# Attention and mixture of experts on one core: the weighted sums of two head groups in one PSUM bank, and the row maxima's transposes at the head of a step

## The chip, the core and the metric

The kernel runs on one core of a Trainium2 chip. The metric is the time of one execution on the device, in microseconds; less is better. A core has a matrix engine (TensorE, PE in the profile, its weight loads PEld), a vector engine (VectorE, DVE), an engine for activation functions (ScalarE, ACT), a general engine (GpSimd, POOL) and SyncE (SP), which here only starts DMA transfers. PE reads SBUF and writes PSUM, which has eight banks of 512 fp32 numbers in each of 128 partitions. The engines run their own queues in order, and wait for each other through semaphores.

## What is computed

Eight sequences of 512 tokens with 128 features. Rows are normalised; the result is the input plus causal attention with 16 heads of 8 dimensions, plus a shared feed-forward block, plus the two best of eight expert blocks for each token.

```python
x = L0_attn_x                       # 8 x 512 x 128
xn = _layernorm(x, axis=-1)
x = x + _L0_attn_ref(xn, ...) + _L0_ffn_ref(xn, ...)

# attention
h = (x @ W1 + b1).reshape(B, S, H, 3 * d)          # H = 16, d = 8
w = einsum('bhqd,bhkd->bhqk', q, k) / sqrt(d)
w = softmax(w * mask - (1 - mask) * 1e6)
a = einsum('bhqk,bhkd->bhqd', w, v)
return a @ Wp + bp

# feed-forward: FF = 352, eight experts, two of them for each token
_ffn = silu(x @ gw.T) * (x @ uw.T) @ dw.T
topw, topi = top_k(softmax(xf @ gate_w.T), 2);  topw = topw / topw.sum()
return shared + sum over experts of _ffn(xf, expert) * its weight
```

## The kernel before

Everything is written out in one order per engine: PE, DVE, ACT and SP take their instructions as the program records them; only POOL's order is left to a scheduler. The 16 heads of a sequence are four groups of four heads, so that there are 32 groups n (`b, g = divmod(n, NG)`). A group is five steps (`TILES`): two "wide" ones, two "mixed" ones and one "half" one, 160 steps in all.

In a step, in this order (the loop at L1092 to L1138):

- `begin(step)` runs what an earlier step has left for the head of this one (the lists in `first`).
- `weigh` fills a pair of banks with scores (`fill`, L308 and the mask's product L312), and ACT takes their exponential into `pT` (L428). From step 33 on and until the routed blocks are done, POOL cuts the causal triangle out of `pT` (L436) in place of the mask's product.
- `look` computes scores for a later group, query rows on the partitions (`peak_scores`, L351 into `sc_left` and `sc_diag`), and DVE reduces them to row maxima (`peaks`, L380 and L386). It is 7 steps ahead at first and 11 from step 24 on. After a group's fifth look, `shift_parts` (L394 to L403) makes of the maxima three bf16 parts.
- `some_chunks` does a chunk of the feed-forward work beside it: `chunk` (two products `gu`, L584; tanh on ACT, L589; two DVE operations `th` and `h`, L590 and L591). There is one PSUM buffer for `gu`.
- `late` holds what the step before has left: `attend`, the weighted sums (L451), and at the end of a group `evacuate` (L475).
- `side` runs what is due in this step (`ready`), then up to two pieces of feed-forward work: `down` (y, L602, copied by ACT to `o`, L610, or added by DVE, L613) or `turn_slots` (s_ps, L568, copied to `sT`, L570).

The weighted sums of a group are four strips of 32 partitions in one bank, `av`: strip jj belongs to head jj of the group. The stationary operand is `v_ext[b % NV][:, c, head, :]`, 32 columns wide: columns 0 to 7 are the head's values, column 8 is 1, so that row 8 of a strip is the softmax's denominator, and columns 9 to 31 are zero. `project_v` copies the values into it, once for each sequence (L277). After a group's last sums, ACT copies the bank to `o_sb` (L475); two steps later `divide` turns it with four transposes (`ot`, L484), and DVE takes the reciprocals of the denominators (`rden`, L486) and multiplies (`a_new`, L490). When a sequence's four groups are divided, `turn` (L498, L499) and `join` (L521, L525) multiply by Wp and add to x.

The maxima's parts go into the query operand as three more rows: `shift` (L409) turns the parts on PE into `mT_ps`, DVE copies them (L411), and `put_shift` starts three DMAs on SP (L416). For groups 4 and up `shift` is due at the second step after the fifth look, in `side`, near the end of that step; `side` then leaves `put_shift` for the head of the next step:

```python
        return lambda: due(step + (2 if n > 3 else 1), partial(shift, n, shift_parts(n)))
```

The products `qk_ps`, `v_ps`, `ot`, `mT_ps`, `y`, `s_ps`, `aT_ps` and `p_ps` share two PSUM buffers of one bank each (`misc`). On SP stand, beside the three DMAs of a shift, the loads of expert weights (L542, 576 KB each, two for a pair of blocks, with six buffers), of the rows of a pair of blocks (L553), and of queries and keys (L285, L287).

The routing is done once, in the first steps; then POOL scatters the rows to the experts' slots (`send`, L649, 64 scatters), and at the end gathers the results (`collect`, L662), which DVE weights and adds (L669). Before the routed blocks and after them the shared block fills the chunks.

Of the kernel before, what the change touches and what calls it, by code (L numbers as in the profile page):

```python
# [11 lines left out]
F32 = mybir.dt.float32  # L12
# [3 lines left out]
ALU = mybir.AluOpType  # L16
# [9 lines left out]
P = 128  # L26
B, S, E = 8, 512, 128
H, D = 16, 8
NC = S // P
NT = B * NC  # L30
NG = H // 4
HH = H // 2
NU = 3
NV = 2
# [28 lines left out]
def attn_moe_kernel(  # L63
# [15 lines left out]
    nc = tc.nc  # L79
# [52 lines left out]
    for i in range(NU):  # L132
        q = const.tile([P, HH, S], BF16, name=f"qs{i}")
        k = const.tile([P, HH, S], BF16, name=f"ks{i}")
# [3 lines left out]
    def ones_below(k):  # L138
        nc.gpsimd.memset(k[64:96].rearrange("p h s -> p (h s)").bitcast(F32), PAIR_OF_ONES)

    ones_below(ks[0])
    for t in v_ext:
        nc.gpsimd.memset(t, 0.0)
        nc.gpsimd.memset(t[:, :, :, D : D + 1], 1.0)


    mask_q = const.tile([P, P], BF16, name="mask_q")
# [48 lines left out]
    def pool(name, bufs, **kw):  # L196
        return ctx.enter_context(tc.tile_pool(name=name, bufs=bufs, **kw))
# [3 lines left out]
    at = pool("at", 2)  # L201
# [68 lines left out]
    def project_v(b):  # L270
        ps = misc([P, NC, H, D], "v_ps")
        for c in range(NC):
            nc.tensor.matmul(
                ps[:, c].rearrange("p h d -> p (h d)"),
                lhsT=xnT[:, ts(b * NC + c, P)], rhs=w1v_sb, start=True, stop=True,
            )
        nc.scalar.copy(v_ext[b % NV][:, :, :, :D], ps)  # L277

    def fetch(u, h0=0, h1=HH):

# [132 lines left out]

    def put_shift(n, mT):
        for r in range(3):
            d = nc.sync.dma_start(  # L416
                qs[n // 2 % NU][QK + r : QK + r + 1, ts(n % 2, 4), :].rearrange(
                    "o h (c s) -> o (h c) s", s=P
                ),
                mT[ts(r, 16)],  # L420
            )
        return d.ins

    def weigh(n, kind, j, on_pool):

# [16 lines left out]
    def attend(n, tiles, av):  # L442

        b, g = divmod(n, NG)

        def add(jj, c, weights):  # L450
            nc.tensor.matmul(  # L451
                av[32 * jj : 32 * jj + 32, c * P :], lhsT=v_ext[b % NV][:, c, 4 * g + jj, :],
                rhs=weights, start=(c == 0), stop=(c == NC - 1), skip_group_check=True,
            )

        heads = [(j + t, pT[:, t]) for _, j, pT in reversed(tiles) for t in range(2)]
        kind = tiles[0][0]
        if kind == "wide":
            for jj, w in heads:
                add(jj, 0, w)  # L460
        elif kind == "mixed":
            for jj, w in heads:
                add(jj, 1, w[:, : 3 * P])
            for jj, w in heads:
                add(jj, 3, w[:, 3 * P :])
        else:
            for t, w in heads:
                for u in range(2):
                    add(2 * t + u, 2, w[:, ts(u, 2 * P)])
# [8 lines left out]
    def divide(n):  # L478

        b, g = divmod(n, NG)  # L480
        o_sb = group_sums.pop(n)
        ot = misc([P, NC, 4, 32], "ot")
        for c in range(NC):
            nc.tensor.transpose(ot[:, c].rearrange("p j s -> p (j s)"), o_sb[:, ts(c, P)], ident)  # L484
        rden = at.tile([P, NC, 4, 1], F32, name="rden")
        nc.vector.reciprocal(rden, ot[:, :, :, D : D + 1])  # L486
        if g == 0:
            a_new = at.tile([P, NC, E], F32, name="a_new")
            a_sb[b] = a_new
        nc.vector.tensor_tensor(  # L490
            a_sb[b][:, :, ts(g, 4 * D)].rearrange("p c (j d) -> p c j d", d=D),
            ot[:, :, :, :D], rden.to_broadcast([P, NC, 4, D]), ALU.mult,
        )

    def turn(b):
# [35 lines left out]
    weights, held, turned, hidden = {}, {}, {}, {}  # L531
# [149 lines left out]
    late = []  # L681
# [3 lines left out]
    def due(step, f):  # L685
        ready.setdefault(step, []).append(f)
# [3 lines left out]
    def look(step, between=lambda: None):  # L690

        t = len(looked)
        if t >= total_steps:
            return lambda: None
        looked.append(step)
        n, i = divmod(t, NTILES)
        maxima(n, i, between)
        if i < NTILES - 1:
            return lambda: None
        if n == 0:  # L700
            return partial(shift_parts, n)
        return lambda: due(step + (2 if n > 3 else 1), partial(shift, n, shift_parts(n)))

    def side(step, most):

# [6 lines left out]
    first = {}  # L712
# [5 lines left out]

    def begin(step):
        for f in first.pop(step, []):  # L720
            f()

    def extra():
        do, more = next(beside, (None, []))
# [325 lines left out]
    for t in range(FIRST):  # L1050
        step = t - FIRST
# [40 lines left out]
    for n in range(B * NG):  # L1092
        b, g = divmod(n, NG)
        waiting = []
        for i, (kind, j) in enumerate(TILES):
            step = n * NTILES + i
            begin(step)
            if step in fetches:
                fetch(fetches[step])
            on_pool = step >= BUSY and len(stored) < NB // MB  # L1100
            waiting.append((kind, j, weigh(n, kind, j, on_pool)))
            parts_then = look(step)
            some_chunks(step, False)
            if step in light:
                warm(5)
            parts_then()
            if step not in MORE and len(looked) < total_steps:
                prepare(*divmod(len(looked), NTILES))
            some_routing()
            for f in late:  # L1110
                f()
            late = []
            if i == 1:
                av = av_ps.tile([P, S], F32, name="av")
            if i in (1, 3, 4):
                late = [partial(attend, n, waiting, av)]
                waiting = []
            side(step, 2)
            some_chunks(step, True)
            if step in MORE:  # L1120
                look(step)()
                prepare(*divmod(len(looked), NTILES))
            if len(stored) == NB // MB:
                for _ in range(2 + (step % 3 == 0)):
                    if gathers:
                        t, i_ = gathers.pop(0)
                        collect(t, i_)
                        due(step + LAG, partial(add_up, t, i_))

                        if i_ and t % NC == NC - 1 and t < MB * EARLY:  # L1130
                            due(max(step + LAG + 1, last_shift), partial(store, t // NC))
        late.append(partial(evacuate, n, av))
        due(step + 2, partial(divide, n))
        if n % NG == 2 and b + 1 < B:
            due(step + 1, partial(offset, b + 1))
        if g == NG - 1:
            due(step + 3, partial(turn, b))
            due(step + 4, partial(join, b))  # L1138
    for f in late:
        f()  # L1140
    while aside or beside is not None:
        do, more = next(beside, (None, []))
# [8 lines left out]
    for step in sorted(ready):  # L1151
        for f in ready[step]:
            more = f()
# [12 lines left out]
def _lay_out(inp):  # L1166

    import numpy as np

    a = {k: np.asarray(v) for k, v in inp.items()}  # L1170
    w1 = a["L0_attn_W1"].reshape(E, H, 3 * D)
    b1 = a["L0_attn_b1"].reshape(H, 3 * D)

    def by_dim(v):
        return np.swapaxes(v, -1, -2).reshape(*v.shape[:-2], D * H)

    def experts(name):
        return np.concatenate([a[f"L0_ffn_expert_{name}"], a[f"L0_ffn_shared_{name}"][None]], axis=0)

    pad = ((0, 0), (0, 0), (0, FP - FF))  # L1180
    w_gate = np.pad(experts("gate").transpose(0, 2, 1), pad)
    w_up = np.pad(experts("up").transpose(0, 2, 1), pad)
    w_down = np.pad(experts("down"), pad)
    w_down = w_down.reshape(NE + 1, E, NF, P).transpose(0, 3, 2, 1).reshape(NE + 1, P, FP)

    arrays = {
        "x": a["L0_attn_x"],
        "w1q": by_dim(w1[:, :, :D]),
        "w1k": by_dim(w1[:, :, D : 2 * D]),
        "bq": by_dim(b1[:, :D]).reshape(P, 1),  # L1190
        "bk": by_dim(b1[:, D : 2 * D]).reshape(P, 1),
        "w1v": w1[:, :, 2 * D :].reshape(E, H * D),
        "bv": b1[:, 2 * D :].reshape(H * D, 1),
        "wp": a["L0_attn_Wp"],
        "bp": a["L0_attn_bp"].reshape(1, E),
        "gate_w": np.pad(a["L0_ffn_gate_w"].T, ((0, 0), (0, GATES - NE))),
        "w_exp": np.concatenate([w_gate, w_up, w_down], axis=2),
    }
    return {f"in_{k}_dram": np.ascontiguousarray(v) for k, v in arrays.items()}
# [17 lines left out]
```

## Time and profile before

| | |
|---|---|
| median of 5 runs | 679.61 us |
| lowest, highest | 677.07, 685.84 us |
| the profiled execution's own time | 678.34 us |
| its span, first to last instruction | 676.6 us |
| mean granted TensorE clock | 0.946 of full speed |
| busy: PE, DVE, ACT, POOL | 575.3, 453.3, 380.2, 240.4 us |
| instructions | 13710 |

The page of the profile gives the busy time of each engine, then the span in 40 slices of 16.9 us with the busy share in tenths, then the chain of work that ended last, then the groups of instructions by line. A group's row reads: line, engine, operation, result <- operands, shapes, count, then the busy time of the group and the mean duration of one in ns, then the time for which the engine had been idle just before them, and for whom it had waited. PE's records overlap, since its matmuls are pipelined: the time from one start to the next start is what one costs, not its duration. An fp32 matmul is recorded as two, a transpose as one. A row of the timeline reads: start, duration, engine, line, what, how many; in brackets how long the engine had been idle before it, and for whom.

### The profile page before, as it was taken

The numbers are of one execution on the slowest core, as the hardware profiler recorded it, in microseconds if no ns is written. First come the engines' busy times: TensorE is split into PE (matmuls) and PEld (weight loads), VectorE is DVE, ScalarE is ACT, GpSimd is POOL, SyncE is SP. The second block draws the span as 40 slices with busy tenths as digits, with TensorE's granted clock in tenths as the row PEclk, the third lists the DMA queues.
The fourth block names the chain that finished last, engine by engine and source line by source line (L and its number), as shares of the span: only waits on it lengthen the run. The fifth ranks groups of instructions, "written<-read, shape, count | busy, mean of one in ns | idle before, by whom it ended". The sixth has DMA issues, their size and how long they took to land.

```text
span 676.6 us, 13710 instructions
## 1 busy us (share of the span) xinstructions
PE 575.3 (85%) x4946; PEld 423.7 (63%) x4946; DVE 453.3 (67%) x1172; ACT 380.2 (56%) x676; POOL 240.4 (36%) x350
## 2 busy tenths in 40 slices
PE   7888892019999999999999989999999999869995
PEld 4564661016767777777777767777877776546653
DVE  7788681017777766767666666677767777769952
ACT  5635351006565666667556675667656676535552
POOL 9313777770000222222222212221222212777750
PEclk9989697559999999999999999999999999969999
DMA  7671532110426668586776659575775723432250
GB/s 201 205 230 72 161 103 74 50 47 25 111 71 143 173 196 219 160 215 185 198 234 182 199 160 208 188 190 182 226 214 176 222 77 87 96 77 54 56 154 16
DMA packets 51533, 98.71 MB, mean 146 GB/s; under 512 B 10137, under 2 KB 35609, under 8 KB 49305
## 3 DMA queue, kind: packets, MB, share of 16 engines
q1 hardware_dynamic: 43912, 79.52, 42.3%
q0 software_dynamic: 6832, 18.23, 8.2%
q8 instruction: 39, 0.64, 0.4%
q14 instruction: 30, 0.24, 0.1%
q10 hardware_dynamic: 720, 0.08, 0.1%
HBM read 73.29 MB, written 24.12 MB: 144 GB/s over the span
## 4 chain that ended last, share of the span: by engine, by line
PE 62%; POOL 11%; DVE 9%; ACT 7%; issue 7%; DMA 3%; SPq 0%; POOLq 0%; DVEq 0%; ACTq 0%
PE gu L584 19%; PE y L602 10%; PE av L451 9%; POOL slots L649 9%; PE scT L308 8%; PE sc_diag L351 4%; PE sc_left L351 4%; DVE peaks L380 2%; PE qk_ps L228 2%; ACT th L589 2%; ACT pT L428 2%; PE s_ps L568 2%; DVE th L590 2%; DMA r<-results,slot 2%; DVE h L591 1%
## 5 line engine op out<-in xcount | busy, mean ns | idle before, releaser
L428 ACT ACTIVATE pT<-scT 128x1024 f32<-128x1024 f32 x160 | 163.8, 1024 | 66.2 <-PE scT L312 52.8
L584 PE MATMUL gu<-sT,w 128*128 128x128 f32 x864 | 116.8, 278 | 13.3 <-DVE h L591 7.9
L436 POOL TENSOR_SCALAR_AFFINE_SELECT pT<-pT 128x256 f32<-128x256 f32 (+1 forms) x130 | 55.1, 436 | 194.3 <-ACT pT L428 194.2
L584 PEld LDWEIGHTS gu<-sT,w 128*128 128x128 f32 x864 | 107.5, 191 | 21.1 <-PE sc_left L351 10.1
L380 DVE TENSOR_REDUCE peaks<-sc_diag 128x4 f32<-128x512 f32 x128 | 87.9, 687 | 46.4 <-PE sc_diag L351 43.1
L308 PE MATMUL scT<-qs,ks 75*128 75x384 bf16 (+3 forms) x512 | 107.4, 304 | 5.5 <-ACT pT L428 5.4
L339 ACT CAST sc_diag<-mask_q 128x512 f32<-128x512 bf16 x117 | 69.3, 592 | 71.2 <-DVE peaks L380 58.6
L590 DVE SCALAR_TENSOR_TENSOR th<-th,gu 128x256 f32<-128x256 f32 x156 | 65.4, 419 | 58.2 <-ACT th L589 56.0
L589 ACT ACTIVATE th<-gu 128x256 f32<-128x256 f32 x156 | 59.8, 383 | 71.7 <-PE gu L584 71.3
L451 PE MATMUL av<-pT,v_ext 128*32 128x512 f32 (+3 forms) x1024 | 90.5, 449 | 0.2 <-ACT pT L428 0.2
L351 PEld LDWEIGHTS <-qs 72*128 72x128 bf16 x896 | 64.9, 99 | 37.7 <-issue 20.9
L380 DVE TENSOR_REDUCE peaks<-sc_left 128x4 f32<-128x512 f32 x128 | 87.1, 681 | 0.0
L649 POOL DMA_INDIRECT slots<-rows_attT,slot x64 | 62.9, 982 | 33.7 <-issue 17.1
L351 PE MATMUL sc_diag<-ks,qs 72*128 72x128 bf16 (+1 forms) x576 | 62.9, 227 | 13.4 <-ACT sc_diag L339 11.9
L591 DVE TENSOR_TENSOR h<-gu,th 128x256 f32<-128x256 f32 x156 | 66.2, 424 | 5.4
L602 PE MATMUL y<-ws_sb,h 128*128 128x128 f32 x192 | 29.7, 294 | 47.0 <-DVE x_sb L613 44.2
L662 POOL DMA_INDIRECT r<-results,slot x64 | 61.3, 958 | 23.1 <-issue 9.9
L602 PE MATMUL y<-w,h 128*128 128x128 f32 x432 | 63.2, 283 | 5.7 <-ACT sT L570 1.6
L602 PEld LDWEIGHTS y<-w,h 128*128 128x128 f32 x432 | 54.2, 191 | 18.5 <-issue 3.9
L351 PE MATMUL sc_left<-ks,qs 72*128 72x128 bf16 (+1 forms) x320 | 62.4, 277 | 3.3 <-DVE peaks L380 3.1
L308 PEld LDWEIGHTS <-ks 75*128 75x128 bf16 x512 | 49.4, 100 | 19.8 <-issue 8.2
L602 PEld LDWEIGHTS y<-ws_sb,h 128*128 128x128 f32 x192 | 25.4, 199 | 54.3 <-DVE x_sb L613 44.4
(159 smaller groups left out, 716.2 us busy)
## 6 DMA issues: line engine op xcount, KB each, us to landing
w<-in_w_exp_dram SPq DMA_DIRECT2D x72, 576.0 KB
qs<-dq SPq DMA_DIRECT2D x45, 192.0 KB
ks<-dk SPq DMA_DIRECT2D x45, 192.0 KB
slots<-zeros POOLq DMA_DIRECT2D x6, 768.0 KB, 5.8
results<-o POOLq DMA_DIRECT2D x36, 128.0 KB, 7.1
s<-slots SPq DMA_DIRECT2D x33, 128.0 KB
dq<-parts SPq DMA_DIRECT2D x7, 384.0 KB
dk<-parts SPq DMA_DIRECT2D x7, 384.0 KB
```

Source lines behind the costliest of these rows:

```text
L308: nc.tensor.matmul(out_, lhsT=k[: QK + 3, ts(i, P)], rhs=q[: QK + 3, i * P :], start=True, stop=bare)
L339: nc.scalar.copy(diag_ps.rearrange("p (b k) -> p b k", k=P), mask_q.unsqueeze(1).to_broadcast([P, NC, P]),)
L351: nc.tensor.matmul(out_, lhsT=q[:QK, ts(c, P)], rhs=k[:QK, keys], start=start, stop=stop, skip_group_check=True,)
L380: nc.vector.tensor_reduce(peaks[:, i, 8 + 4 * t : 12 + 4 * t], banks[t].rearrange("p (b k) -> p b k", k=P), AX.X, ALU.max,)
L428: nc.scalar.activation(pT, ps, AF.Exp, scale=D**-0.5)
L451: nc.tensor.matmul(av[32 * jj : 32 * jj + 32, c * P :], lhsT=v_ext[b % NV][:, c, 4 * g + jj, :], rhs=weights, start=(c == 0), stop=(c == N ...
L584: nc.tensor.matmul(gu[:, i, part], lhsT=w[c][:, ds(i * FP + f * P, P)], rhs=sT[:, part], start=True, stop=True,)
L589: nc.scalar.activation(th, gu[:, 0], AF.Tanh, scale=0.5)
L590: nc.vector.scalar_tensor_tensor(th, th, 1.0, gu[:, 0], ALU.add, ALU.mult)
L591: nc.vector.tensor_tensor(h[:, f], gu[:, 1], th, ALU.mult)
L602: nc.tensor.matmul(y, lhsT=h[:, f, ts(c, P)], rhs=w[c % len(w)][:, ds(2 * FP + f * P, P)], start=(f == 0), stop=(f == NF - 1),)
L649: d = nc.gpsimd.indirect_dma_start(slots, bass.IndirectOffsetOnAxis(ap=slot[:, i, t : t + 1], axis=0), rows[:, t, :], None,)
```

## The change

One bank now holds the sums of two groups. Groups with an even number write into it as before; for odd groups the values stand 16 columns further right in `v_ext`, so that their sums and denominator come into rows 16 to 24 of each strip, and the zero columns add nothing to the rows of the other group. The bank is opened by the even group's first matmul and closed by the odd group's last. It is copied to `o_sb` and divided once for two groups, after the odd one: four transposes, one reciprocal of 128x32 and one product of 128x256 in place of twice four, two of 128x16 and two of 128x128. The order of the heads in the result changes with it, and `bv` and `wp` are laid out to match on the host (`by_sums`). The values are copied into `v_ext` by two copies of 128x256 in place of one of 128x512, and the ones are set by two memsets for each of the two `v_ext` in place of one.

For groups 4 and up the shift is put at the head of the step in whose `side` it was due: transpose, copy and the three DMAs are all recorded in `begin`.

```diff
+    def halves_of(t):
+        return t.rearrange("p c (q t j) s -> p (c q) t j s", t=2, j=4)
...
-        nc.gpsimd.memset(t[:, :, :, D : D + 1], 1.0)
+        for i in range(2):
+            nc.gpsimd.memset(halves_of(t)[:, :, i, :, 16 * i + D : 16 * i + D + 1], 1.0)
...
-        nc.scalar.copy(v_ext[b % NV][:, :, :, :D], ps)
+        for i in range(2):
+            nc.scalar.copy(
+                halves_of(v_ext[b % NV])[:, :, i, :, 16 * i : 16 * i + D], halves_of(ps)[:, :, i]
+            )
...
-                rhs=weights, start=(c == 0), stop=(c == NC - 1), skip_group_check=True,
+                rhs=weights, start=(n % 2 == 0 and c == 0), stop=(n % 2 == 1 and c == NC - 1),
+                skip_group_check=True,
...
-        ot = misc([P, NC, 4, 32], "ot")
+        ot = misc([P, NC, HH, 16], "ot")
         for c in range(NC):
-            nc.tensor.transpose(ot[:, c].rearrange("p j s -> p (j s)"), o_sb[:, ts(c, P)], ident)
-        rden = at.tile([P, NC, 4, 1], F32, name="rden")
+            nc.tensor.transpose(ot[:, c].rearrange("p k s -> p (k s)"), o_sb[:, ts(c, P)], ident)
+        rden = at.tile([P, NC, HH, 1], F32, name="rden")
         nc.vector.reciprocal(rden, ot[:, :, :, D : D + 1])
-        if g == 0:
+        if g == 1:
...
-            a_sb[b][:, :, ts(g, 4 * D)].rearrange("p c (j d) -> p c j d", d=D),
-            ot[:, :, :, :D], rden.to_broadcast([P, NC, 4, D]), ALU.mult,
+            a_sb[b][:, :, ts(g // 2, HH * D)].rearrange("p c (k d) -> p c k d", d=D),
+            ot[:, :, :, :D], rden.to_broadcast([P, NC, HH, D]), ALU.mult,
...
-        return lambda: due(step + (2 if n > 3 else 1), partial(shift, n, shift_parts(n)))
+        if n < 4:
+            return lambda: due(step + 1, partial(shift, n, shift_parts(n)))
+        return lambda: first.setdefault(step + 2, []).append(partial(shift, n, shift_parts(n)))
...
         for f in first.pop(step, []):
-            f()
+            more = f()
+            if more is not None:
+                more()
...
-            if i == 1:
+            if i == 1 and n % 2 == 0:
                 av = av_ps.tile([P, S], F32, name="av")
...
-        late.append(partial(evacuate, n, av))
-        due(step + 2, partial(divide, n))
+        if n % 2:
+            late.append(partial(evacuate, n, av))
+            due(step + 2, partial(divide, n))
```

More of the change, by code (lines that the diff above doesn't have):

```diff
@@ L415, in put_shift @@
         for r in range(3):
-            d = nc.sync.dma_start(
+            nc.sync.dma_start(
                 qs[n // 2 % NU][QK + r : QK + r + 1, ts(n % 2, 4), :].rearrange(
@@ L421, in put_shift @@
             )
-        return d.ins
     def weigh(n, kind, j, on_pool):
@@ L1170, in _lay_out, with by_sums @@
     a = {k: np.asarray(v) for k, v in inp.items()}
+    def by_sums(v):
+        return v.reshape(2, 2, 4, D, -1).transpose(0, 2, 1, 3, 4).reshape(H * D, -1)
     w1 = a["L0_attn_W1"].reshape(E, H, 3 * D)
@@ L1192, in _lay_out @@
         "w1v": w1[:, :, 2 * D :].reshape(E, H * D),
-        "bv": b1[:, 2 * D :].reshape(H * D, 1),
-        "wp": a["L0_attn_Wp"],
+        "bv": by_sums(b1[:, 2 * D :]),
+        "wp": by_sums(a["L0_attn_Wp"]),
         "bp": a["L0_attn_bp"].reshape(1, E),
```

## The prediction

> **What bounds the kernel now.** I read the page's head and its forty slices first, then the chain that ended last, then the groups by line, and last the timeline around single steps.
>
> ```profile
> span 676.6 us, 13710 instructions
> PE 575.3 (85%) x4946; PEld 423.7 (63%) x4946; DVE 453.3 (67%) x1172; ACT 380.2 (56%) x676; POOL 240.4 (36%) x350
> ...
> PE   7888892019999999999999989999999999869995
> ```
>
> A slice is 16.9 us. TensorE (PE) is nearly full from 149 to 570 us, and hardly works from 105 to 149 us. The chain says why:
>
> ```profile
> 139.53 0.97 POOL slots L649
> ...
> 149.38 1.65 PE y L602 x6
> ...
> 587.41 7.85 DMA r<-results,slot
> ```
>
> So there are three stages. **A**, to 149 us: the chain runs through the 64 scatters on POOL (L649), which start at 59.7 us, when the routing is done; what PE saves before 149 us is lost in the 44 us for which it then waits. **B**, 149 to 570 us: PE's own work sets the pace. **C**, 570 to 677 us: gathers, DVE, ACT and PE in turn. The groups that the change touches:
>
> ```profile
> L484 PE MATMUL ot<-ident,o_sb 128*128 128x128 f32 x128 | 19.4, 274 | 0.5 <-ACT v_ext L277 0.5
> L475 ACT COPY o_sb<-av 128x512 f32<-128x512 f32 x32 | 18.8, 587 | 1.2 <-PE av L451 1.2
> L490 DVE TENSOR_TENSOR a_new<-ot,rden 128x128 f32<-128x128 f32 x32 | 9.3, 292 | 1.1
> L486 DVE RECIPROCAL rden<-ot 128x16 f32<-128x16 f32 x32 | 8.0, 249 | 0.6 <-PE ot L484 0.4
> L277 ACT COPY v_ext<-v_ps 128x512 f32<-128x512 f32 x8 | 4.6, 578 | 0.0
> ```
>
> That PE is full does not mean that each instruction taken off it returns its time. Two stretches of PE's timeline in B, for groups 9 and 18:
>
> ```profile
> 281.00 1.05 PE L584 MATMUL gu<-sT,w 128*128 128x128 f32 x8
> 281.89 0.60 PE L484 MATMUL ot<-ident,o_sb 128*128 128x128 f32 x4
> 282.33 0.83 PE L602 MATMUL y<-w,h 128*128 128x128 f32 x6
> 283.54 1.13 PE L584 MATMUL gu<-sT,w 128*128 128x128 f32 x8 [0.37 <-DVE h L591]
> ...
> 459.40 0.60 PE L484 MATMUL ot<-ident,o_sb 128*128 128x128 f32 x4
> 459.83 0.83 PE L602 MATMUL y<-w,h 128*128 128x128 f32 x6
> 460.50 0.60 PE L308 MATMUL scT<-qs,ks 75*128 75x384 bf16 x4
> 461.39 1.06 PE L584 MATMUL gu<-sT,w 128*128 128x128 f32 x8
> ```
>
> The four transposes of a division hold PE for 0.44 us (281.89 to 282.33). But there is one PSUM buffer for gu, so the next gu must wait until DVE has read the last one (h, L591). At 283.54 PE waited for that, and it started 0.15 us after h ended (282.97+0.42). There the transposes only fill a gap. At 461.39 h had ended at 460.89, 0.50 us before, so PE could start at most 0.35 us earlier.
>
> **The change, part by part.** One division now serves an even and the following odd group, at the odd one's time. Gone are 16 divisions, those of even groups: on PE 64 transposes, on ACT 16 copies o_sb of 587 ns (9.4 us), on DVE 16 x (249+292) = 8.7 us, of which the larger odd divisions take back part: no row shows a reciprocal of 128x32 out of PSUM; L947's 128x32 took 353, and L591's product of 128x256 with PSUM took 424, so one pair costs 777 for 1082, 4.9 us less in all. The sums' matmuls (L451) keep number and shape; they wrote all 32 rows of a strip before too.
>
> *Stage A.* The divisions of groups 0 and 2 go (59.6 and 104.6 us): nothing, since the scatters cover it. The ones in v_ext need four memsets for two; the row L144 is 218 ns for 64 elements, the smallest near row 147 ns; if two more stand on POOL's way to the first rows (13.85 us) that is 0.3 us later, but POOL then idles 0.6 us for DVE at 16.59. I take +0.2, bounds 0 and +0.4.
>
> *Stage B, divisions.* Ten go, groups 4, 6, ... 22. The ceiling is 10 x 0.44 = 4.4. By the slack between h's end and the next gu: group 4 has 0.38, so 0.23; 6, 8, 16, 18, 20 and 22 have 0.50, so 6 x 0.35 = 2.1; 10 waits as group 9 does, so 0; 12 and 14 have 1.79, so 2 x 0.44. In these two a second y waits 0.35 for the copy of the first, as ot holds the other buffer of the two; ot gone, that goes too: 0.7. Sum 3.9. Without ot the cover for h's latency is gone, which is why 4.4 is not reached.
>
> *Stage B, ACT.* The o_sb copy of group 14 (397.78) stands ahead of parts and sT, and y at 399.21 waits 1.16 for sT: without the copy 0.6 less. Other o_sb copies hide behind PE work. The v_ext copy becomes two of 128x256; L570 has that shape out of PSUM, 375 ns, so 750 for 578, +0.17. PE waits for this copy at 245.49, 321.68, 403.48, 480.78 and 556.30: +0.9. At 172.56 it is ot that waits 0.55, and in the built order of the changed kernel ot takes the other buffer there: -0.3. Net +0.6, bounds 0 and +1.2.
> [...]
>
> *Stage B, the maxima's parts.* For groups from 4 on, the transpose mT (L409, 0.17 us from its start to the next matmul), its copy on DVE (L411, 207) and the three DMAs (L416) move from the end of step s+2 and the start of s+3 to the start of s+2. Gain: y at 420.02 and 438.40 waits 0.41 for mT's buffer; mT turned a step's work earlier, that is 0.8. Loss: at 338.99, 357.70 and 376.43 gu waits after mT, which filled a gap, and the 0.17 now stands in full PE work: 0.5. A new wait: on PE the fills of scT (L308), the peak scores (L351) and so ACT's exp stand behind mT, which needs one of two buffers. In the built order five of the 28 moved mT take a buffer that was filled one or two products before, and wait for ACT's copy (265 ns, with s_ps's 0.22 to 0.28 between): some 0.1 each, 0.5 in all; bounds 0, and 5 x 0.6 = 3 if a cast of 592 is ahead of that copy. DVE's copy stands ahead of the peaks (L380), for which DVE idles about 1 us at that place: free; without that cover it would cost 28 x 0.2 = 5.8. On SP the three DMAs (587 ns each to issue) pass the weight loads of the step, which then stand behind them: the load issued at 273.81 would go at about 279.9, and is used at 290.07, 10 us later. Loads issued 4.5 us ahead (325.00 for 329.52) made no one wait: free.
>
> B sums to -3.9 -0.6 +0.6 -0.8 +0.5 +0.5 = -3.7.
>
> *Stage C.* Group 24's division lies ahead of the gathers (the 7.85 us above), which hide it. From 600 to 640 us DVE is busy 35.9 of 40; group 26 takes 0.54 off it, 28 half as much, the larger odd 27 adds 0.24: -0.6. Group 30's transposes (658.72) stand before a fill that waits 0.72 for ACT's exp anyway: 0. The last division is on the path to the end (ot 668.78, aT 670.05), and longer by 0.1+0.13: +0.2. C: -0.4; bounds -2 and +0.5.
>
> **Sum.** +0.2 -3.7 -0.4 = -3.9: span 672.7. The profiled execution took 678.34 for a span of 676.6, so 674.4; the median of the runs shown, 679.61, is 1.3 above it, so 675.7, 0.6% faster. About 1% is what a measurement of this kernel tells from no change (its five runs lie between 677.07 and 685.84).
>
> **Rivals.**
> *Every removed transpose counts.* If gu's wait for h shrinks as well, because ACT and DVE have less ahead of th and h, the 14 even groups from 4 to 30 return 14 x 0.44 = 6.2, and with the waits (0.7+0.6+0.8) and none of the losses -8.3, some +0.4 at both ends: 671.7. For: PE is 9 tenths full in B. Against: 283.54, where the chain gu, th, th, h has nothing ahead of it and is still the longer.
> *All in gaps.* The gain of the divisions goes into waits for h, and the new waits eat the rest: -2.1 (y, sT, mT) +0.5 +0.5 +0.6, and +0.4 at both ends, about 0: 679.5. For: 14 rows in B where gu waits 0.37 to 0.60 for h. Against: the slack of 0.35 in six groups.
> *mT at the head of the step stalls PE.* If most of the 28 wait for an ACT copy that stands behind an exp (1024 ns), as L428 does run at the turn of steps, 14 of them at 1.0 cost 14 in place of the 0.5: 689.2. It decides against the change from 3.9/28 = 0.14 us each. Against: most of the 28 take a buffer emptied a step before.
> *Weight loads held behind the DMAs of the shift.* If the 10 us left shrink to less than a load takes, gu waits for w: at 1 us in each of 14 groups, 675.7 + 14 = 689.7. Against: the 4.5 us above.
>
> **Chances.** Forecast 0.50, all in gaps 0.20, every transpose 0.20, mT stall 0.06, weight loads 0.04. Faster by over 1% (below 672.8): most of "every transpose" (671.7) and a little of the forecast, 0.22; slower by over 1%: nearly all of the last two, 0.09; the rest 0.69. Range 670.0 to 680.5: from a little below "every transpose" to a little above "all in gaps"; the stalls of the last two stay outside.
>
> **What would show it.** In the changed profile: ot x64, o_sb x16, rden 128x32 near 353, a_new 128x256 near 424, v_ext x16 near 375. The stretch from the first PE work after the scatters to the last result stored shortens by 3 to 5 us, while its start stays within 0.5 us of 149.4. gu keeps its waits for h of 0.37 to 0.60, and they grow at even groups; y's waits for mT and, at groups 12 and 14, for o are gone; y's waits for v_ext grow to about 0.4 to 0.5. I am wrong if PE waits at mT for over 1.5 us in all, if any gu waits for a weight DMA, or if the start of B moves by over 1 us.

## The result, and the profile after

The changed kernel takes 675.67 us in the median (671.22 to 681.69), the kernel before 678.50 over the 86 runs measured beside it (675.45 to 685.84, but for one of 1907.85). The ratio is 0.9963, with a 95% interval of 0.9953 to 0.9974: 0.4% faster, which lies within the 1% that the prediction called no change. The prediction was 675.7, but that it fits to 0.03 us is luck: it stood for 3.9 us less than 679.61, the median of five runs. Over 86 runs the kernel before has 678.50, so the measured difference is 2.83 us. The profiled execution took 676.01 us, 2.33 less than that of before.

The page's head, slices and chain of the changed kernel:

```profile
span 674.3 us, 13541 instructions
...
PE 571.9 (85%) x4882; PEld 416.2 (62%) x4882; DVE 450.6 (67%) x1140; ACT 372.4 (55%) x668; POOL 240.4 (36%) x352
...
PE   6888793009999999999999999999999999879885
```

```profile
61.48 1.05 POOL slots L658
...
150.80 0.30 DVE x_sb L622
...
151.14 0.27 PE mT_ps L418
...
583.67 8.09 DMA r<-results,slot
```

The three stages are there as before, but the first is longer: scatters start at 61.48 us (59.72 before), and PE resumes at 151.14 (149.38). The groups by line are those that were named ahead:

```profile
L493 PE MATMUL ot<-ident,o_sb 128*128 128x128 f32 x64 | 9.6, 273 | 0.0
L484 ACT COPY o_sb<-av 128x512 f32<-128x512 f32 x16 | 9.4, 586 | 1.0 <-PE av L459 1.0
...
L499 DVE TENSOR_TENSOR a_new<-ot,rden 128x256 f32<-128x256 f32 x16 | 6.8, 425 | 0.5
...
L495 DVE RECIPROCAL rden<-ot 128x32 f32<-128x32 f32 x16 | 5.6, 350 | 0.2
...
L284 ACT COPY v_ext<-v_ps 128x256 f32<-128x256 f32 x16 | 5.1, 372 | 0.0
```

The two stretches of PE's timeline, for groups 9 and 18. Group 9 is odd and keeps its transposes; those of group 18 are gone:

```profile
282.77 0.60 PE L493 MATMUL ot<-ident,o_sb 128*128 128x128 f32 x4
283.21 0.83 PE L611 MATMUL y<-w,h 128*128 128x128 f32 x6
284.42 1.13 PE L593 MATMUL gu<-sT,w 128*128 128x128 f32 x8 [0.37 <-DVE h L600]
...
456.29 0.83 PE L611 MATMUL y<-w,h 128*128 128x128 f32 x6
456.96 0.60 PE L317 MATMUL scT<-qs,ks 75*128 75x384 bf16 x4
...
457.63 0.38 PE L360 MATMUL sc_left<-ks,qs 72*128 72x128 bf16 x2
457.93 1.13 PE L593 MATMUL gu<-sT,w 128*128 128x128 f32 x8
```

Group 9 keeps its wait of 0.37 too. At group 18 gu now starts 0.30 us after sc_left, where before it was 0.22 (461.17 to 461.39): it has begun to wait for h, so the 0.44 of the transposes come back only in part.

**One ruler for all kernels.** Every kernel here has the same 156 chunks, each with one tanh on ACT (th). The distance from the 19th to the 139th (171.00 to 562.37 us before) covers nearly all of stage B, whatever happens ahead of it, and the gain of an edit can be read at each chunk: over most of that stretch two kernels keep their distance to within 0.02 us from one chunk to the next (at 74 of the 120 steps between before and after, at 107 between before and the kernel with half the loads), and it jumps where they differ. The kernels are those of the experiments below; all in us. "Scatter" is the start of the first one; "19th to 139th" is the distance itself for the kernel before, and the difference to it for the others; "tail" runs from the 139th tanh to the end:

| kernel | scatter | 19th tanh | 19th to 139th | tail | profiled time | median |
|---|---|---|---|---|---|---|
| before | 59.72 | 171.00 | 391.37 | 114.23 | 678.34 | 678.50 |
| before again | 59.55 | 171.07 | +0.33 | 114.23 | 678.70 | |
| after | 61.48 | 171.72 | -3.03 | 114.24 | 676.01 | 675.67 |
| after again | 63.66 | 176.56 | -2.46 | 113.93 | 681.18 | 676.48 |
| pairs only | 60.10 | 170.74 | -3.30 | 113.49 | 674.38 | 678.03 |
| shift only | 60.53 | 174.09 | +0.10 | 114.64 | 681.92 | 680.92 |
| idle transposes | 59.84 | 171.76 | -0.78 | 115.05 | 679.14 | 681.16 |
| idle copies | 61.51 | 174.43 | -3.11 | 112.61 | 677.05 | |
| three turns | 59.71 | 170.70 | -6.66 | 115.59 | 673.10 | 675.88 |
| one v copy | 63.22 | 176.16 | -7.01 | 114.98 | 677.60 | 675.96 |
| PE kept awake | 61.67 | 175.18 | -6.00 | 112.75 | 675.39 | 674.34 |
| first four single | 60.31 | 171.22 | +1.05 | 114.46 | 680.02 | 675.56 |
| half the loads | 60.25 | 171.76 | -6.94 | 115.81 | 673.92 | 675.30 |

So in the two profiles shown the change brings 3.03 us in B, loses 0.72 ahead of it and nothing behind. (The prediction's own mark, from the first PE work after the scatters to the last result stored, goes from 420.8 to 416.6; but PE did one y of 1.4 us ahead of the wait in the changed kernel, so this 4.2 is not all gain.) A profiled execution is one run, and not always a typical one: pairs only, with 674.38, was profiled in the fastest of its 12 runs, the changed kernel's second profile, with 681.18, is the slowest of 12. So only the stretch is compared between profiles, and the time between medians.

### The profile page after: what moved, and what is told of

The parts are those of the page before. It is cut to its first block, busy times and chain, and to the rows that moved or that the text cites. A ratio compares the mean times of both kernels' runs of the same rounds, so it can differ in the third digit from the quotient of the medians.

```text
span 674.3 us, 13541 instructions
## 1 busy us (share of the span) xinstructions
PE 571.9 (85%) x4882; PEld 416.2 (62%) x4882; DVE 450.6 (67%) x1140; ACT 372.4 (55%) x668; POOL 240.4 (36%) x352
## 4 chain that ended last, share of the span: by engine, by line
PE 63%; POOL 11%; DVE 8%; ACT 7%; issue 6%; DMA 4%; SPq 1%; DVEq 0%; POOLq 0%; ACTq 0%
PE gu L593 19%; PE av L459 10%; PE y L611 9%; POOL slots L658 9%; PE scT L317 8%; PE sc_diag L360 4%; PE sc_left L360 4%; PE qk_ps L234 2%; DVE peaks L389 2%; ACT th L598 2%; ACT pT L436 2%; PE s_ps L577 2%; DVE th L599 2%; ACT sc_diag L348 1%; DVE h L600 1%
## 5 line engine op out<-in xcount | busy, mean ns | idle before, releaser
L317 PEld LDWEIGHTS <-ks 75*128 75x128 bf16 x512 | 48.0, 100 | 66.9 <-issue 54.0
L626 POOL DMA_DIRECT2D results<-o x36 | 26.1, 724 | 87.0 <-ACT o L619 79.5
L593 PE MATMUL gu<-xnT,ws_sb 128*128 128x256 f32 x192 | 54.3, 408 | 0.3 <-DVE h L600 0.3
```

Source lines behind the costliest of these rows:

```text
L317: nc.tensor.matmul(out_, lhsT=k[: QK + 3, ts(i, P)], rhs=q[: QK + 3, i * P :], start=True, stop=bare)
L593: nc.tensor.matmul(gu[:, i, part], lhsT=w[c][:, ds(i * FP + f * P, P)], rhs=sT[:, part], start=True, stop=True,)
```

## The experiments

**Pairs only, shift only.** The two halves of the change. Pairs only has the shift as before:

```diff
-        if n < 4:
-            return lambda: due(step + 1, partial(shift, n, shift_parts(n)))
-        return lambda: first.setdefault(step + 2, []).append(partial(shift, n, shift_parts(n)))
+        return lambda: due(step + (2 if n > 3 else 1), partial(shift, n, shift_parts(n)))
```

> The changed kernel with the shift at its old place: only the sums of two groups in one bank. Theory: the divisions bring nearly all of it, and the moved shift is worth -0.8 +0.5 +0.5 = +0.2 us by the prediction's terms; measured in the changed kernel's trace the lost fillers are 3 x 0.17 = 0.5 and the waits for mT 0.4, so between 0.1 and 0.5 us are to be won by putting it back: the time is within 0.6 us of the changed kernel's. y's waits of 0.41 for mT come back, gu's slack of 0.33 instead of 0.50 too, and loads of expert weights are issued as early as in the kernel before, so that no gu waits for them. Rival: the moved shift carries the gain, and this kernel takes the time of the kernel before (2.5 us more than the changed one).

Shift only is the kernel before with the lines that are taken away here.

> The kernel before with only the shift of groups 4 and up put at the head of its step. Theory: within 0.6 us of the kernel before. Rival 1: the moved shift carries the gain: 2 to 2.5 us faster. Rival 2: it costs, because loads of expert weights are issued behind its DMAs and gu waits for some of them, or PE waits for mT's buffer: 1 us slower or more, and pairs alone are then that much faster than the changed kernel.

Measured: pairs only 0.9985 of before (0.9964 to 1.0007), shift only 1.0047 (1.0025 to 1.0070). In the time, 0.6 us at most was expected of each. Shift only misses it: it is 2.28 us above the kernel before (680.92 against 678.64). Pairs only is 1.55 above the changed kernel measured in the same round (678.03 against 676.48), but their intervals overlap (0.9941 to 0.9983 for the latter). Nor do the two medians add up to that of the change. In the stretch between the tanhs the two are -3.30 and +0.10, and there the changed kernel, with -3.03, is close to their sum. Three places account for what differs, to within 0.1: a late load in the changed kernel (0.39, below), 0.22 at group 4 that either half wins but both together only once, and 0.37 at one gu that shift only loses and the changed kernel doesn't. What shift only's one profile loses stands ahead of the stretch: 113.56 us from the first scatter to the 19th tanh in place of 111.28. Whether that makes its median is not shown.

The shift's small net hides two large sums. It gains 1.58 + 0.83 + 0.84 = 3.25 at groups 17, 18 and 19, and gives 3.35 back over all others. First the gain, PE's timeline before and after:

```profile
397.45 0.24 PE L409 MATMUL mT_ps<-ident,m_parts 128*48 128x128 bf16 x1
397.62 0.44 PE L568 MATMUL s_ps<-ident,s 128*128 128x128 f32 x2
399.21 0.94 PE L602 MATMUL y<-w,h 128*128 128x128 f32 x6 [1.16 <-ACT sT L570]
399.98 0.60 PE L308 MATMUL scT<-qs,ks 75*128 75x512 bf16 x2
```

```profile
397.51 0.44 PE L577 MATMUL s_ps<-ident,s 128*128 128x128 f32 x2
397.79 0.83 PE L611 MATMUL y<-w,h 128*128 128x128 f32 x6
398.46 0.60 PE L317 MATMUL scT<-qs,ks 75*128 75x512 bf16 x2
```

mT held one of the two `misc` buffers and s_ps the other, so y had to wait until ACT had copied s_ps. With mT turned earlier y finds a free one. From mT (or s_ps) to scT it is 2.53 before and 0.95 after: 1.58 us. The row's 1.16 is less than what the wait cost, for three reasons that the rows show: 0.17 is mT itself; 0.15 lies between the next possible start, 0.28 after s_ps, and the recorded end, from which the idle time is counted; and a y that has waited takes 0.77 to the next start where one without a wait takes 0.67.

Now a place where the shift costs, pairs only and after:

```profile
258.72 0.94 PE L611 MATMUL y<-w,h 128*128 128x128 f32 x6
259.49 0.60 PE L317 MATMUL scT<-qs,ks 75*128 75x512 bf16 x2
```

```profile
260.05 0.94 PE L611 MATMUL y<-w,h 128*128 128x128 f32 x6
260.92 0.24 PE L418 MATMUL mT_ps<-ident,m_parts 128*48 128x128 bf16 x1
261.09 0.60 PE L317 MATMUL scT<-qs,ks 75*128 75x512 bf16 x2
```

At the head of the step mT costs 0.27, its 0.17 and 0.10 ahead of it; at the old place 0.17 come back, or nothing where mT had filled a gap. For a group this makes 0.1 to 0.3 in most cases and up to 0.5 in a few. Five of the moved mT wait for their buffer, four for 0.11 to 0.14 and one for 0.38 (471.45, for ACT's o).

**Four idle transposes put back.**

```diff
         if n % 2:
             late.append(partial(evacuate, n, av))
             due(step + 2, partial(divide, n))
+        else:
+            due(step + 2, fill_in)   # four transposes of the identity
```

> The changed kernel with four transposes put back on PE at the place where an even group was divided (of the identity, into a buffer that nobody reads; no copy on ACT and no work on DVE). What they cost is what PE's transposes were worth. Theory (they count where the time from the end of h to the next gu leaves no gap): 0.23 + 6 x 0.35 + 2 x 0.44 = 3.2 us in the stretch from the first PE work after the scatters to the last result stored, and 0.7 more if the waits of the second y at groups 12 and 14 come back with the second buffer. Rival 1, every transpose counts: 10 x 0.44 = 4.4 or more there. Rival 2, all in gaps: under 1 us; then the gain came from the copies on ACT and the work on DVE.

Measured: 1.0029 of before (1.0007 to 1.0051), and -0.78 in the stretch where the changed kernel has -3.03. The jumps: 0.27 at each of the six groups 6, 8, 16, 18, 20 and 22, 0.14 once more near group 6, 0.45 and 0.43 at groups 12 and 14, none at 4 and 10 (at 4 the moved mT has left a gap: in the changed kernel sc_diag waits 0.26 for ACT at 193.30): 2.63 in all, of which 0.39 is hidden in the total, because a late load in the changed kernel (below) was not late here. That is between the rivals, and close to the theory's 3.2. Groups 12 and 14 gain 1.06 each in the other kernels with pairs and lose only 0.45 and 0.43 of it here: the remaining 0.6 is the second y, which finds a buffer:

```profile
342.56 0.60 PE L484 MATMUL ot<-ident,o_sb 128*128 128x128 f32 x4
343.00 0.83 PE L602 MATMUL y<-w,h 128*128 128x128 f32 x6
344.19 0.94 PE L602 MATMUL y<-w,h 128*128 128x128 f32 x6 [0.35 <-ACT o L610]
344.96 0.60 PE L308 MATMUL scT<-qs,ks 75*128 75x384 bf16 x4
```

```profile
344.19 1.50 PE L611 MATMUL y<-w,h 128*128 128x128 f32 x12
345.53 0.60 PE L317 MATMUL scT<-qs,ks 75*128 75x384 bf16 x4
```

2.40 before, 1.34 after, and again the wait's price (0.62) is above its row (0.35).

**ACT's copies and DVE's work put back.** An idle copy of the bank after each even group, and two products of the old sizes on it.

> The changed kernel with ACT's copy of the bank put back after even groups, and two products on DVE of the size of the old reciprocal and the old product (on the copy, result unused); no transposes. Theory: ACT's and DVE's part of the division was worth nothing between 171 and 562 us (there PE is the bound, and the kernel with pairs alone still shows y waiting 1.16 us for sT with the copy of group 14 gone), so that stretch is as long as the changed kernel's to within 0.3 us, and the 3.0 us it gains are transposes and PSUM buffers. Rival, the prediction's own terms: the copy of group 14 brings its 0.6 back. After 570 us DVE's 0.5 to 0.8 us come back in the stretch to the end.

Measured: -3.11 in the stretch, and -3.42 is what the changed kernel has without its late load. So ACT's 16 copies and DVE's 32 operations are worth 0.3 us there, all of them together, and it stands at one place: a gu at 433.67 waits 0.35 for DVE's h. In shift only, which has these copies and operations too, the same wait stands at 435.84. The kernel before, with the copies but the old shift, doesn't have it (433.20), nor does the changed kernel, with the new shift but no copies (430.64): it takes both. The tail is 112.61, the shortest of all, so DVE's part of stage C can't be seen among tails that lie between 112.6 and 115.8.

**The changed kernel again, and the kernel before again.** Nothing is changed in either.

> The changed kernel once more, unchanged, for a second profile. In the first one PE resumed after the scatters at 151.14 us instead of 149.38. Theory: 0.4 of these 1.76 us are a weight load that took longer and most of the rest is a lower granted clock of PE at 40 to 50 us, both of which differ between executions, so a second profile puts the start anywhere from 148.5 to 152, with the stretch behind it the same to within 1 us. Rival: the change does it (two more memsets, other places of the first divisions), and the start is 151.1 again to within 0.3.

> The kernel before once more, for a second profile of the time ahead of the scatters. Theory (pairs in the first sequence lengthen the stretch of half clock): the scatters start within 1 us of 59.7 us again. Rival (chance): anywhere from 59.7 to 63.7 us. From 171 to 562 us it is the first profile to within 0.3 us, unless a load of weights is late.

The changed kernel resumed at 153.33, later still than 151.14 and outside of the range that was given; the same program moved by 2.2 us. The kernel before started its scatters at 59.55. The difference follows PE's granted clock, and the change isn't its cause: the kernel with idle transposes has the changed kernel's program up to 59.80 us, and starts its scatters at 59.84. Windows of the changed kernel's first and second profile (window, sum, busy time of PE, PEld, DVE, ACT, POOL with instructions, granted clock, DMA share, GB/s):

```profile
42.00:46.00 4.00, 3.44 (x25) 2.18 (x26) 3.76 (x14) 1.54 (x2) 2.14 (x4) 0.53 0.44 174
46.00:50.00 4.00, 4.00 (x28) 1.84 (x21) 3.21 (x10) 1.30 (x2) 0.00 (x0) 0.62 1.02 412
50.00:54.00 4.00, 4.00 (x60) 3.56 (x57) 1.49 (x4) 1.75 (x3) 0.00 (x0) 1.00 0.52 206
...
155.00:159.00 4.00, 4.00 (x30) 2.32 (x30) 2.40 (x5) 2.28 (x4) 0.00 (x0) 1.00 0.03 6
```

```profile
42.00:46.00 4.00, 3.08 (x25) 2.07 (x27) 3.76 (x13) 1.54 (x2) 2.14 (x4) 0.66 0.40 154
46.00:50.00 4.00, 4.00 (x23) 1.74 (x19) 2.97 (x10) 1.17 (x2) 0.00 (x0) 0.50 1.03 412
50.00:54.00 4.00, 4.00 (x29) 3.27 (x28) 1.20 (x2) 1.03 (x2) 0.00 (x0) 0.56 0.58 230
...
155.00:159.00 4.00, 4.00 (x18) 1.85 (x16) 2.66 (x7) 1.90 (x3) 0.00 (x0) 0.50 0.02 3
```

From 42 us on the clock was at half for 6.8 us in the one (42.3 to 49.1) and 10.3 in the other (43.2 to 53.5), and after the wait for the scatters until 154.9 and 159.3. The other profiles fit: with none or 3.4 us of half clock at 40 to 54 us the scatters start at 59.55 to 60.53, with 6.8 at 61.48 and 61.67, with 10.3 at 63.22 and 63.66. One doesn't (idle copies, 3.4 us and 61.51). The lengths come in steps: 6.8 and 10.3 are two and three times the 3.4 of the kernel before (41.0 to 44.4). What sets the size of the step, and why one execution has more of them than another, is not shown.

**Only the turns that gain, and one copy for v_ext.** The shift at the head for three groups; then also v_ext's values at columns 16 to 23 for every head, with the window of weights moved in place of the values:

```diff
+        at_step = step + (2 if n > 3 else 1)
+        if n not in (17, 18, 19):
+            return lambda: due(at_step, partial(shift, n, shift_parts(n)))
+        return lambda: first.setdefault(at_step, []).append(partial(shift, n, shift_parts(n)))
...
+        nc.scalar.copy(heads_of(v_ext[b % NV])[:, :, :, 16 : 16 + D], ps)
...
+            at_ = 32 * (H * c + 4 * g + jj) + 16 * (1 - n % 2)
...
+                lhsT=v_ext[b % NV][:, at_ : at_ + 32],
```

> The changed kernel with the shift at the head of its step for groups 17, 18 and 19 only, where the trace shows y behind mT's buffer gone (399.21, 420.02, 438.40 of the kernel before); for all others it is at its old place. Chunk by chunk between 171 and 562 us, pairs alone gain 3.3 us on the kernel before, the shift alone loses 0.1: it wins 1.58 + 0.83 + 0.84 at these three groups and gives the same back at the others, 0.1 to 0.7 at a time. Theory: the two parts add up place by place, so this kernel gains 3.3 + 3.25 = 6.5 us in that stretch, and takes about 672 us. Rival: the stall of these three y only goes to the next wait when the other turns are not moved with them, and the kernel is as fast as pairs alone (3.3 us in that stretch).

> As the kernel with three turns, and the values go into v_ext in one copy of 128x512 again: they stand at columns 16 to 23 of each head's 32, with the one at column 24, and the weights of the sums' matmuls are taken as 32 columns from the head's first (odd groups) or from its seventeenth (even groups, which end in the zeros of the next head). Theory: the second copy cost 0.05 to 0.07 us at each of the five y behind it in the trace, so 0.3 us less from 171 to 562 us than with two copies. Rival: the prediction's own price, 0.17 at each of five, 0.9 less. In the time neither can be told from the kernel with three turns.

Measured in the stretch: -6.66 and -7.01. The parts add up place by place, and the second copy of v_ext costs 0.35, not 0.9. ACT's rows of before and after show why:

```profile
402.85 0.58 ACT L277 COPY v_ext<-v_ps 128x512 f32<-128x512 f32 x1
```

```profile
401.32 0.65 ACT L284 COPY v_ext<-v_ps 128x256 f32<-128x256 f32 x2
```

Two copies with a mean of 372 ns are over after 0.65, since they overlap by 0.1. That is 0.07 more than the one copy, and the products that wait for it come 0.06 later, six times in the stretch. The medians, however, are 675.88 and 675.96 (ratios 0.9981, 0.9955 to 1.0006, and 0.9964, 0.9936 to 0.9993), where 672 was expected for the first.

**Where the rest of these 6.7 us went.** Four attempts. PE kept busy through the wait for the scatters:

> As the kernel with one copy for v_ext, and PE does 96 idle products (identity by shared weights, 128x256 fp32, into the bank pair that the next fill overwrites) while it waits for the scatters. In six profiles the granted clock was 0.50 from the end of that wait on, for 3.1 to 7.9 us. Theory: the clock is 1.00 when PE resumes, so PE is 1.5 to 4 us earlier by 171 us, counted from the end of the scatters, and the time is lower by about 2 us and spreads less. Rival: the half clock after the wait hides behind ACT and DVE, which work off their own queues then, and nothing is won; or the idle products end after the scatters and cost time.

```profile
148.99 0.22 PE L321 MATMUL scT<-mask_k,ident 128*128 128x128 bf16 x1
152.56 0.58 PE L360 MATMUL sc_diag<-ks,qs 72*128 72x128 bf16 x4 [3.36 <-ACT sc_diag L348]
```

PE still idled 3.36 us after the idle products, and the clock was at half from 151.9 to 158.7 us. From the first scatter to the 19th tanh it took 113.51 us, 111.28 in the kernel before: nothing is won at that place. (Its -6.00 in the stretch holds one late load of weights, 0.91 at the 73rd tanh.) The median, 674.34, is the lowest of all (0.9942, 0.9921 to 0.9964; 673.24 to 676.30), for a reason that the one profile doesn't show.

The first four groups without pairs, then the same with more idle products:

```diff
+    def opens(n):
+        return n < NG or n % 2 == 0
+    def closes(n):
+        return n < NG or n % 2 == 1
...
+                rhs=weights, start=(opens(n) and c == 0), stop=(closes(n) and c == NC - 1),
```

> As the kernel with three turns and one copy for v_ext, but groups 0 to 3 (the first sequence, whose sums lie in the time ahead of the scatters) have a bank and a division of their own again, as in the kernel before; pairs from group 4 on. The chunks say that the kernel with three turns is 6.7 us shorter than the kernel before from 171 to 562 us, yet its median is only 2.3 lower, and its 12 runs fall into two clumps, 673 to 677 and 678 to 680. Theory: what is lost lies ahead of the scatters, where the granted clock is at half in one stretch from about 40 us on for anything from 0 to 10 us (scatters start at 59.7 to 63.7 us), and pairs in the first sequence make the long stretch likelier. Then this kernel starts its scatters by 60.5 us, loses the upper clump, and its median is about 671.5. Rival: the long stretch comes by chance in any of these kernels, and the kernel takes the 676 us of the kernel with three turns, in two clumps again.

> As the kernel with the first four groups single, and 103 idle products on PE in the wait for the scatters (96 ended 3.4 us before the wait did, and the clock was at half from 152 to 158 us all the same). Theory: with under 1 us left idle the clock stays at 1.00 through the end of the wait, and the stretch from the first scatter to the chunk at 171 us, 111.3 us in the kernel before, is 1.5 to 3 us shorter. Rival: nothing is won there, since ACT and DVE work off the same steps at their own pace.

The scatters start at 60.31, but the median is 675.56 (0.9952, 0.9930 to 0.9975) with the upper clump still there, so the 671.5 and the clump's end, which the theory foretold, didn't come. For the stretch at 42 to 53 us it could not have held: the first instruction in which this kernel differs from the one with pairs everywhere is ACT's o_sb copy at 57.45. The second kernel is a plain miss: with the first four single, PE waits at a y that stands ahead of the idle products, which then ran after the wait and cost their 44 us (719.21):

```profile
150.02 1.65 PE L625 MATMUL y<-ws_sb,h 128*128 128x128 f32 x6 [44.32 <-DVE x_sb L636]
```

What the profile of the first four single did show is a second thing that moves the time: late loads of weights. In its timeline and its chain:

```profile
463.87 1.50 PE L602 MATMUL gu<-sT,w 128*128 128x128 f32 x6 [1.24 <-DMA w<-in_w_exp_dram]
```

```profile
451.45 12.38 DMA w<-in_w_exp_dram
...
531.22 9.36 DMA w<-in_w_exp_dram
```

Six chunks are later by 8.05 us in all, four of them with such a wait. The other two follow on the first and the third wait, behind each of which the clock was at half for 3.4 us (272.9 to 276.3 and 464.1 to 467.5). Without the six the stretch would be the same -7.0; the kernel with the 103 idle products, whose profile has no late load, is at -6.97 there. So the loads were halved:

> As the kernel with the first four groups single, but of the two loads of expert weights for a pair of blocks only the first is made, and the second block uses the first one's weights (the result is that of other experts for these blocks; all products, copies and other transfers stay). In the profile of the kernel with the first four single, gu is later by 1.36, 1.22, 0.58, 2.85, 0.92 and 1.12 us at six chunks, in four of which it waits for a load; without these 8.05 the stretch from 171 to 562 us would be 7.0 us shorter than in the kernel before. Theory: loads that come late in some executions are what keeps the median at 675.6 and makes the clump of 677 to 680. Then this kernel has no such chunk, is 7.0 us shorter in that stretch, and its median is 671 to 672.5 with no run above 676. Rival: the clump is the half clock ahead of the scatters and at the gathers; then the median stays within 1 us of 675.6 and the clump stays.

Measured: -6.94 in the stretch and no wait for a load; the runs end at 677.81 instead of 680.02; but the median is 675.30 (0.9947, 0.9925 to 0.9969). Late loads may account for the slowest executions, not for the median; there the rival holds.

So the medians of the timed kernels other than the changed one lie some 2 to 4.5 us above what their stretch promises, those of pairs only, shift only and idle transposes too. The mean granted clock of each run, which is on record beside its time, gives a part of the answer. In pairs only the time follows it closely: the two runs at 0.950 took 674.38 and 674.78 us, the three at 0.938 and 0.939 took 679.99 to 681.80. With three turns it is 673.09 to 673.32 at 0.946 to 0.948 and 676.74 to 680.30 at 0.936 to 0.939. In the kernel with the first four single it is not so (672.27 and 680.02 us, both at 0.948), which leaves room for the late loads. Why the clock is lower in more runs of one kernel than of another stays open, and so does the rest of the 2 to 4.5 us. Seen in single profiles: scatters from 59.6 to 63.7 us, half clock after the wait for 3 to 8 us, tails from 112.6 to 115.8 with 7 to 14 us of half clock between 588 and 609 us, and 1.9 to 2.1 us outside of the span in place of 1.7 (for instance 673.10 against 671.0 with three turns). No version is shown to beat the changed kernel: the best interval, 0.9921 to 0.9964, overlaps with 0.9953 to 0.9974.

## Why the prediction was right, and which of its steps were not

- **Time.** 675.7 foretold, 675.67 measured. The way and the size are right, the last digit is luck: the change was foretold at -3.9 and is -2.83 by the medians, with a start that five runs had put 1.1 too high. B was foretold at -3.7 and is -3.03 by the tanhs (-2.46 in the second profile). That is near because wrong terms offset each other; only the divisions came, in sum, as worked out. In the profiles -3.03 in B and +0.72 ahead of it make the -2.33; that the medians' -2.83 has the same parts is not shown, since the medians of the two halves don't add up to it.
- **Divisions, -3.9.** Right: -0.22 at group 4, six times -0.27, nothing at group 10, twice -1.06: -3.96. The rule of slack held, with 0.27 for 0.35 (gu waits 0.08 for h and then takes 1.06 for 0.98 to the next start). The two y's were priced 0.35 by their rows and were worth 0.62. In the whole change the -0.22 at group 4 is won only once, by the division or by the moved mT. "Every transpose counts" and "all in gaps" are both refuted by the idle transposes (2.63 us).
- **ACT, the copy of group 14, -0.6.** Wrong: the copy at 397.78 is that of group 15, an odd one, and is still there in the changed kernel (0.59 at 397.84); pairs only has y's wait of 1.16 unchanged. The expectation of the idle copies repeats that slip. The wait went away through the moved mT, with 1.58.
- **v_ext, +0.6.** Too high: 0.06 at each of the five y's and 0.06 at the ot behind the 19th tanh, +0.36 with pairs only, since two copies in a row overlap. The row's 0.17 took the second copy as additional in full (2 x 375 for 578 ns), where the two together take 0.65 us for 0.58. The -0.3 for that ot did come, but by the moved mT: in the changed kernel ot finds the other buffer (172.41, no wait), which is worth -0.27 in shift only and in the changed kernel. A gap ahead of the first s_ps grew by 0.24 in every kernel with pairs, which was not foreseen; its cause stays open.
- **The maxima's parts, +0.2.** Net +0.10, but from -3.25 and +3.35 in place of -0.8 and +1.0. The failed step is "0.17 in three gaps": each mT at the head costs 0.27, and only 0.17 comes back at most places. The 0.10 that PE loses ahead of each was put at nothing. The new waits were foretold in number (five) and for four of them in size (0.11 to 0.14); the fifth, 0.38, brings them to 0.87 for 0.5. Neither stalls as in the third rival were seen, nor a cost of DVE's copy by itself. The net +0.10 holds the -0.27 of ot and the 0.37 that shift only loses at one gu.
- **SP's loads, free.** Not quite. gu did wait: the load issued at 454.35 took 7.25 us in the chain, and the chunk behind it is 0.39 later, in the second profile 0.99. (The prediction had named such a wait a sign of being wrong.) The idle transposes, with the same place of the shift, have no wait there, and the kernel with the first four single, with the old place, has the worst. So it is the duration of a load in one execution that decides; that the moved DMAs add to it was not separated. The kernel before has a jump of 0.26 in its second profile (a gu of 1.39 in place of 1.13 at 503.94), for which the trace names no wait.
- **A, +0.2, and C, -0.4.** Neither can be told. PE's resumption moved by 1.76 us, which the prediction had named a sign of being wrong; but it differed by 2.2 us between two profiles of one program, so that "moves by over 1 us" was no test of the change. The tails differ by 3.

## What to carry to other kernels

Split a change and compare the parts chunk by chunk, at a mark that every kernel has: a net of 0.1 us was 3.25 won and 3.35 lost, and the places of the two told which turns to move. Price a wait by the distance of the starts around it, not by the idle time of its row (0.41 was 0.66, 0.35 was 0.62, 1.16 was 1.41, each without mT), and check to which group an instruction belongs before you count it as removed. Before you follow a start that moved between two profiles, take a second profile of the same kernel.

## What the hardware showed that was not expected

- The stretch in which PE is the bound repeats to 0.02 us at most chunks between executions, and between two profiles of one kernel it moved by one jump (0.26 in the kernel before, at a gu whose wait the trace doesn't name; 0.60 in the changed one, at a late load). The start of the scatters, in the stage before, spread from 59.55 to 63.66 us.
- Loads of 576 KB took 5.3 to 12.4 us in the chain where gu waited for one.
- Two ACT copies out of PSUM in a row overlap by 0.1 us (372 ns each, 0.65 together).
- PE resumed at half clock after an idle stretch of only 3.36 us (152.56), and the full clock came 6.1 us later (158.7).
